# Two-layer graph network with two expert mixtures: the fused middle pass re-ordered, its answers halved on VectorE, weight loads moved and marked

## The chip, the cores and the metric

One core of one Trainium2 chip. The metric is the device time of one execution in microseconds (us), given as the median of three. Everything is float32; matrix products of the network run on the matrix engine (TensorE, PE), and the vector engine (VectorE, DVE), the scalar engine (ScalarE, ACT), GpSimd (POOL) and the DMA queues (SyncE's, written SPq, ScalarE's, written ACTq, and GpSimd's) feed it.

## What is computed

`x` holds 128 graphs of 64 nodes with 256 features, 8192 tokens in all, and `adj` an adjacency matrix of 64 x 64 for each graph. Cut to what matters, with `ln` a layer norm without weights:

```
# layer 0
n  = ln(x)
a  = epsilon*n + adj @ n
x1 = x + silu(rmsnorm(a @ W1 + b1)) @ W2 + b2          # 256 -> 1024 -> 256
n1 = ln(x1)
s, i = softmax_top6(n1 @ gate_w.T)                      # 6 of 64 experts for each token
m  = sum_k s_k * (n1 @ lattice[i_k])                    # each expert 256 x 256
x2 = x1 + layernorm(n1 + m @ out_w.T + out_b) * ln_g + ln_b
# layer 1
n2 = ln(x2)
h  = layernorm(n2) * gamma + beta
x3 = x2 + n2 + relu((adj @ h) @ W_rel + b_rel + h @ W_root)
n3 = ln(x3)
top2 of 8 experts by n3 @ Wg + bg + bias
out = x3 + sum over the 2 of w_e * (relu(n3 @ W1_e + b1_e) @ W2_e + b2_e)
```

## The kernel before

The tokens are cut into 32 blocks of 256 (`NB`), each held as two tiles of 128 rows (`T` = 2) with 256 columns (`KD` = 2 halves of 128). The kernel has four parts.

**First stage** (lines 496 to 727), one pass over the blocks: graph network of layer 0, gate, the six choices of each token. A `Router` gives each (token, choice) pair a row in a table in DRAM, and `send` writes the rows there with indirect DMAs from GpSimd. Memory is short: the tile `lat`, which will hold the 64 lattice experts, lends its upper 28 experts to this stage (weights, hidden values, x). `load_lattice` stands in the list for blocks 8 to 23 and fills the lower part, two experts (512 KB) a block; the rest is loaded after the stage. `load_late` issues the loads of constants and of W2 in the first step.

**Lattice pages** (729 to 782): 424 pages of 128 rows are fetched from the table, transposed, multiplied by the page's expert, scaled by the softmax weight and written by indirect DMA to the array `r0.answer`, six rows (`K0`) for each token.

**Fused pass** (785 to 998), where most of the change lies, one pass over the blocks. For each block:

- `load3` loads the six answers of each token as `y` (128 rows x 2 x 6 x 256), and the stored `xn1`, `x1` and adjacency.
- `mixture` transposes the answers on TensorE and adds the six in PSUM as it does so: 2 halves x 2 tiles x 6 answers = 24 transposes (line 828). ScalarE copies the sum to `accT`.
- `out_proj` multiplies by `out_w` into the PSUM tile `po` (lines 836, 839); `layer_out_h` adds `xn1` to it on VectorE and so frees `po` (845).
- `layer_out_a` takes mean and variance of `h` and lets ScalarE take the root (`spread`, line 36); `layer_out_b` normalises `h`, applies `ln_g`, adds `x1` (860, 862) and takes the statistics of the result `x2`; `layer_out_c` makes `hn` and `s` of it on ScalarE (879, 883).
- `flip_h` transposes `hn`; `neighbours` multiplies by `W_rel` (`pz`, 900) and ScalarE copies it to `z` (903); `convolve_a` adds bias and `W_root` product (`pc`, 908, 911); `convolve_b` applies the adjacency to `z` (917).
- `residual1_a` forms `x3` and its statistics (923); `residual1_b` normalises it twice over into `xs`; `flip3` and `gate1` transpose it and compute the gate (line 76, 946), ScalarE copying between them (940).
- `choose1` takes the two best experts (952 and on), `count1` counts the rows of each expert with small products (191), and `place1` computes the row numbers and sends `xs`.

**Expert pages** (1001 to 1060): 69 pages of 256 rows through the second mixture, added onto the output by indirect DMA.

The order of the work inside a pass is written out by hand. `staggered(n, stages)` runs step by step; in step s it calls each entry (lag, f) of a list, in the order of the list, for block s - lag. So in one step `mixture` works on block s+1 while `choose1` works on block s-3. TensorE, VectorE and ScalarE execute in exactly the order in which this produces the instructions (`manual_schedule`); the DMA queues of SyncE and the work of GpSimd are ordered by a scheduler that looks at what is ready.

PSUM of the fused pass: three rotating tiles `ps` for transposes, and one each of `po`, `pz`, `pc`, `pg` (gate) and `pos` (counts). A tile with one buffer is written again only when its reader is done. The list of the fused pass before:

```
(-2, load3), (0, layer_out_h), (3, choose1), (-1, mixture), (1, flip_h), (3, count1),
(2, residual1_a), (0, layer_out_a), (-1, out_proj), (2, residual1_b), (1, neighbours),
(0, layer_out_b), (1, convolve_a), (2, flip3), (1, convolve_b), (2, gate1),
(3, place1), (0, layer_out_c), (4, load_w2)
```

Of the kernel before, what the change touches and what calls it, by code (L numbers as in the profile page):

```python
# [9 lines left out]
F32 = mybir.dt.float32  # L10
# [5 lines left out]
AF = mybir.ActivationFunctionType  # L16
ALU = mybir.AluOpType
AX = mybir.AxisListType
PSUM = bass.MemoryType.PSUM
P = 128  # L20


def rows_of(vec, n=P):

    return bass.AP(tensor=vec.tensor, offset=vec.offset, ap=[[0, n], [1, vec.shape[0]]])
# [377 lines left out]
def staggered(n, stages, first=0):  # L403

    for s in range(first + min(lag for lag, _ in stages), n + max(lag for lag, _ in stages)):
        for lag, f in stages:
            if first <= s - lag < n:
                f(s - lag)
# [3 lines left out]
def two_layer_gnn_moe_kernel(ctx: ExitStack, tc: tile.TileContext, a: dict, out: bass.AP):  # L412
    nc = tc.nc
    x_in, adjT = a["x"], a["adjT"]
    N, D = x_in.shape
# [4 lines left out]
    T = 2  # L420
    C = T * P
# [4 lines left out]
    K0 = 6  # L426
# [14 lines left out]
        nc.gpsimd.memset(eps[v], v)  # L441
    ops = Ops(nc, small, ident, eps)

    def load_rows(pool, name):
        t = pool.tile([P, a[name].shape[0]], F32, name="r_" + name)
        nc.scalar.dma_start(out=t, in_=rows_of(a[name]))
        return t

    def load_columns(pool, name):

        t = pool.tile([P, a[name].shape[0] // P], F32, name="c_" + name)
        with nc.allow_non_contiguous_dma(reason="small vector"):
            nc.scalar.dma_start(out=t, in_=a[name].rearrange("(c p) -> p c", p=P))
        return t

    def load_matrix(pool, name):

        t = pool.tile([P, a[name].shape[0] // P, a[name].shape[1]], F32, name="m_" + name)
        nc.scalar.dma_start(out=t, in_=a[name].rearrange("(k p) f -> p k f", p=P))
        return t  # L460

    def row_parts(rest, name):
# [14 lines left out]
    def by_tile(ap):  # L477
        return ap.rearrange("(t p) d -> p t d", p=P)
# [8 lines left out]
    def load_adjacency(b):  # L487
        at = adjacency[b % 4]
        for g in range(2):
            nc.sync.dma_start(out=at[g * G:(g + 1) * G, :, g * G:(g + 1) * G],  # L490
                              in_=adjT[2 * b * T + g:2 * (b + 1) * T:2].rearrange("t m n -> m t n"))
        return at
# [3 lines left out]
    r0 = Router(tc, const, small, dram, N, D, E0, K0, T, P, 14 * P, 4, "r0")  # L496
# [3 lines left out]
    lat = lat_pool.__enter__().tile([P, E0, KD, D], F32, name="lat")  # L500
# [18 lines left out]
    with tc.tile_pool(name="c0", bufs=1) as c0, \  # L519
# [9 lines left out]
        blocks = [dict() for _ in range(NB)]  # L529
# [14 lines left out]
        w1 = w1_view.rearrange("p c n -> p (c n)").rearrange("p (k f) -> p k f", k=KD)  # L544
        nc.scalar.dma_start(out=w1, in_=a["L0_gnn_W1"].rearrange("(k p) f -> p k f", p=P))
        b1 = load_columns(c0, "L0_gnn_b1")
        w2 = w2_view
        late = {}

        def load_late(b):  # L550

            if b == 0:
                late["L0_gnn_b2"] = load_rows(c0, "L0_gnn_b2")
                late["rms_w"] = load_columns(c0, "L0_gnn_rms_weight")
                nc.scalar.dma_start(out=w2, in_=a["L0_gnn_W2"].rearrange("(k p) f -> p k f", p=P))
                late["gate_wT"] = load_matrix(c0, "L0_ffn_gate_wT")
                for name in ("L0_ffn_out_b", "L1_gnn_b_rel"):
                    late[name] = load_rows(c0, name)

        def split_late(b):  # L560
            if b < 3:
# [124 lines left out]
        def load_lattice(b):  # L686
            n = free[0] // 16
            if 8 <= b < 24:
                nc.sync.dma_start(out=lat[:, (b - 8) * n:(b - 7) * n], in_=lat_w[:, (b - 8) * n:(b - 7) * n])

        nc.scalar.preload_act_table_set("natural_log_exp_and_others")
# [18 lines left out]
            (0, square_sum),  # L710
            (-1, aggregate),
            (-1, load_late),
            (1, lambda b: project(b, 0, 4, KH)),
            (2, turn),
# [3 lines left out]
            (2, gate),  # L718
            (0, scale),
            (1, load_lattice),  # L720
        ))
        r0.page_table(sq.rearrange("p c n -> p (c n)"))
        n = free[0] // 16
# [65 lines left out]
    with tc.tile_pool(name="c3", bufs=1) as c3, \  # L789
            tc.tile_pool(name="work3", bufs=2) as work, \  # L790
            tc.tile_pool(name="ps3", bufs=3, space=PSUM) as psum, \
            tc.tile_pool(name="po3", bufs=1, space=PSUM) as po_pool, \
            tc.tile_pool(name="pm3", bufs=1, space=PSUM) as pmix:
        out_wT = load_matrix(c3, "L0_ffn_out_wT")
        ln_g = load_rows(c3, "L0_ffn_ln_g")
        ln_b = load_rows(c3, "L0_ffn_ln_b")
        gamma = load_columns(c3, "L1_gnn_ln_gamma")
        beta = load_columns(c3, "L1_gnn_ln_beta")
        w_rel = load_matrix(c3, "L1_gnn_W_rel")
        w_root = load_matrix(c3, "L1_gnn_W_root")  # L800
        wg = load_matrix(c3, "L1_ffn_Wg")
# [5 lines left out]
        blocks = [dict() for _ in range(NB)]  # L807
        pg = pmix.tile([P, T, E1], F32, name="pg")
        r1.begin(counts, work, pmix.tile([P, 2, T, E1], F32, name="pos"))

        def load3(b):
            B = blocks[b]
            B["y"] = y = work.tile([P, T, K0, D], F32, name="y")
            nc.sync.dma_start(out=y, in_=r0.answer[ts(b, C * K0), :].rearrange("(t p k) d -> p t k d", p=P, k=K0))
            B["xn1"] = xn1 = work.tile([P, T, D], F32, name="xn1", bufs=3)
            nc.sync.dma_start(out=xn1, in_=by_tile(xn1_dram[b]))
            B["x1"] = x1 = work.tile([P, T, D], F32, name="x1", bufs=3)
            nc.sync.dma_start(out=x1, in_=by_tile(x1_dram[b]))
            B["at"] = load_adjacency(b)

        def mixture(b):

            B = blocks[b]
            pt = psum.tile([P, KD, C], F32, name="ps")
            for k in range(KD):
                for t in range(T):
                    for i in range(K0):
                        nc.tensor.matmul(pt[:, k, ts(t, P)], lhsT=B["y"][:, t, i, ts(k, P)], rhs=ident,  # L828
                                         start=(i == 0), stop=(i == K0 - 1), is_transpose=True)
            B["accT"] = accT = work.tile([P, KD, C], F32, name="accT", bufs=1)  # L830
            nc.scalar.copy(accT, pt)

# [14 lines left out]
        def layer_out_a(b):  # L847
# [2 lines left out]
            B["rsh"] = ops.spread(B["mvh"])  # L850
            nc.vector.tensor_add(B["x1"], B["x1"], ln_b.unsqueeze(1).to_broadcast([P, T, D]))

        def layer_out_b(b):
            B = blocks[b]
            h = B["h"]
            mv, rs = B["mvh"], B["rsh"]
            nc.vector.reciprocal(rs, rs)
            B["x2"] = x2 = work.tile([P, T, D], F32, name="x2")
            for t in range(T):
                nc.vector.scalar_tensor_tensor(h[:, t, :], h[:, t, :], mv[:, t, 0:1], ln_g,  # L860
                                               op0=ALU.subtract, op1=ALU.mult)
                nc.vector.scalar_tensor_tensor(x2[:, t, :], h[:, t, :], rs[:, t:t + 1], B["x1"][:, t, :],
                                               op0=ALU.mult, op1=ALU.add)
            B["mv2"] = mv = ops.stats(x2)
            B["std2"] = ops.spread(mv)


            B["rs2"] = rs2 = small.tile([P, T], F32, name="rs2")
            ops.std(rs2, mv[:, :, 1], 1e-10, 1.0 + 1e-5)
# [93 lines left out]
        def place1(b):  # L963
            B = blocks[b]
            r1.send(r1.places(b, B["hot"]), B["xs"])

        staggered(NB, (
            (-2, load3),
            (0, layer_out_h),
            (3, choose1),  # L970
            (-1, mixture),
            (1, flip_h),
            (3, count1),
            (2, residual1_a),
            (0, layer_out_a),
            (-1, out_proj),
            (2, residual1_b),
            (1, neighbours),
            (0, layer_out_b),
            (1, convolve_a),  # L980
            (2, flip3),
            (1, convolve_b),
            (2, gate1),
            (3, place1),
# [103 lines left out]
```

## Time and profile before

| | before |
|---|---|
| time, median of 3 (lowest, highest) | 2461.87 us (2459.57, 2465.52) |
| the execution on the page | 2187.6 us, granted TensorE clock 0.959 |
| TensorE busy | 1947.8 us (89%) |
| VectorE busy | 1183.7 us (54%) |
| ScalarE busy | 1014.9 us (46%) |
| GpSimd busy | 1182.9 us (54%) |

| part of the kernel | TensorE from, to (us) | a unit of work |
|---|---|---|
| first stage | 9.9 to 650.3 | 32 blocks |
| lattice pages | 692.3 to 1222.1 | 424 pages |
| fused pass | 1257.7 to 1648.6 | 32 blocks |
| expert pages | 1660.8 to the end | 69 pages |

The timed executions took some 274 us longer than the one that the profiler recorded; the page covers the latter only. "Busy" is an average over four parts with different limits, so a stretch of one part says more than the first lines of the page. A group of instructions is written as line, engine, operation, output<-inputs, count, then busy time and mean of one, then the idle time of the engine just before and what ended it. The granted clock is 1.00 at full speed; 0.50 means that the matrix engine ran at half of it.

### The profile page before, as it was taken

The numbers are of one execution on the slowest core, as the hardware profiler recorded it, in microseconds if no ns is written. First come the engines' busy times: TensorE is split into PE (matmuls) and PEld (weight loads), VectorE is DVE, ScalarE is ACT, GpSimd is POOL, SyncE is SP. The second block draws the span as 40 slices with busy tenths as digits, with TensorE's granted clock in tenths as the row PEclk, the third lists the DMA queues.
The fourth block names the chain that finished last, engine by engine and source line by source line (L and its number), as shares of the span: only waits on it lengthen the run. The fifth ranks groups of instructions, "written<-read, shape, count | busy, mean of one in ns | idle before, by whom it ended". The sixth has DMA issues, their size and how long they took to land. (4 is left out here: it accounts for less than half of the span.)

```text
span 2185.7 us, 37432 instructions
## 1 busy us (share of the span) xinstructions
PE 1947.8 (89%) x10563; PEld 1686.4 (77%) x10564; DVE 1183.7 (54%) x3904; ACT 1014.9 (46%) x2037; POOL 1182.9 (54%) x1178
## 2 busy tenths in 40 slices
PE   5999999999943989998899389999986999999997
PEld 4887888888842877877777278888875888888886
DVE  4888888888873333333333258888882222222221
ACT  3887787778730222222222046666652333333332
POOL 1267666666665777777777603333343344334444
PEclk8999999999975999999999789999997999999999
DMA  8243333333365988667665379788835766666765
GB/s 250 79 133 130 134 132 134 128 132 132 118 215 166 278 255 253 206 205 205 206 206 167 100 286 310 261 260 264 267 119 152 178 157 168 159 153 164 163 159 118
DMA packets 283580, 398.93 MB, mean 183 GB/s; under 512 B 56024, under 2 KB 237416, under 8 KB 283376
## 3 DMA queue, kind: packets, MB, share of 16 engines
q1 hardware_dynamic: 200736, 246.15, 38.2%
q0 software_dynamic: 64800, 136.14, 20.9%
q10 hardware_dynamic: 17840, 14.21, 2.1%
q8 instruction: 93, 1.52, 0.3%
q14 instruction: 111, 0.91, 0.1%
HBM read 223.89 MB, written 177.69 MB: 184 GB/s over the span
## 5 line engine op out<-in xcount | busy, mean ns | idle before, releaser
L287 POOL DMA_INDIRECT r0x<-xs,r0row x384 | 398.5, 1038 | 209.7 <-issue 96.0
L294 POOL DMA_INDIRECT r0y<-py_s,px x424 | 417.5, 985 | 143.4 <-DMA r0y<-py_s,px 56.7
L768 PE MATMUL py<-lat,pxT 128*128 x1696 | 412.0, 386 | 40.8 <-DVE py_s L773 23.4
L773 DVE TENSOR_SCALAR py_s<-py,px 128x256 f32<-128x256 f32 x424 | 185.5, 479 | 376.8 <-DMA r0y<-py_s,px 152.2
L302 POOL DMA_INDIRECT out_x<-py_s,px x138 | 214.3, 1553 | 312.4 <-DMA out_x<-py_s,px 244.4
L768 PEld LDWEIGHTS py<-lat,pxT 128*128 128x128 f32 x1696 | 307.6, 191 | 92.9 <-ACT pxT L755 29.2
L755 ACT COPY pxT<-pt 128x512 f32<-128x512 f32 x212 | 123.8, 586 | 440.5 <-PE pt L753 342.0
L1027 ACT ACTIVATE phid<-ph,pw 128x256 f32<-128x256 f32 x276 | 130.7, 474 | 325.1 <-issue 181.6
L1025 PE MATMUL ph<-pxT,pw 128*128 128x256 f32 x1104 | 251.7, 381 | 1.7 <-DMA pw<-in_L_ffn_W1b 1.7
L1044 PE MATMUL py<-fw,phid 128*128 x1104 | 249.9, 379 | 0.3 <-issue 0.3
L599 PE MATMUL ph<-lat 128*128 128x256 f32 x1024 | 233.4, 387 | 17.9 <-DVE lat L621 17.2
L632 PE MATMUL ps<-lat 128*128 128x256 f32 x1024 | 237.5, 380 | 0.0
L1025 PEld LDWEIGHTS ph<-pxT,pw 128*128 128x128 f32 x1104 | 211.2, 191 | 31.1 <-ACT pxT L1016 2.0
L599 PEld LDWEIGHTS ph<-lat 128*128 128x128 f32 x1024 | 195.3, 193 | 47.4 <-DVE lat L621 17.5
L1044 PEld LDWEIGHTS py<-fw,phid 128*128 128x128 f32 x1104 | 204.4, 190 | 25.6 <-issue 0.5
L632 PEld LDWEIGHTS ps<-lat 128*128 128x128 f32 x1024 | 193.1, 191 | 24.6
L287 POOL DMA_INDIRECT r1x<-xs,r1row x128 | 129.6, 1012 | 116.7 <-ACT xn3T L940 62.7
L753 PE MATMUL pt<-ident,px 128*128 128x128 f32 x848 | 131.1, 278 | 43.1 <-DMA px<-r0x 42.7
L753 PEld LDWEIGHTS pt<-ident,px 128*128 128x128 f32 x848 | 107.1, 143 | 67.7 <-issue 43.2
L1038 DVE TENSOR_SCALAR p<-p 128x2 f32<-128x2 f32 x69 | 12.7, 184 | 242.8 <-ACT p L1037 242.8
L1047 DVE TENSOR_TENSOR py_s<-py,pb 128x512 f32<-128x512 f32 x69 | 47.7, 692 | 156.4 <-PE py L1044 151.4
L828 PE MATMUL ps<-ident,y 128*128 128x128 f32 x768 | 93.7, 281 | 38.6 <-DMA y<-r0y 38.6
(264 smaller groups left out, 2874.4 us busy)
## 6 DMA issues: line engine op xcount, KB each, us to landing
px<-r0x SPq DMA_DIRECT2D x424, 129.0 KB
y<-r0y SPq DMA_DIRECT2D x32, 1536.0 KB
pw<-in_L_ffn_W1b SPq DMA_DIRECT2D x69, 514.0 KB
px<-r1x SPq DMA_DIRECT2D x69, 258.0 KB
x<-x SPq DMA_DIRECT2D x64, 256.0 KB
pb<-in_L_ffn_b SPq DMA_DIRECT2D x69, 128.0 KB
r0x<-r0filler ACTq DMA_DIRECT2D x64, 129.0 KB
lat<-in_x SPq DMA_DIRECT2D x32, 256.0 KB
```

Source lines behind the costliest of these rows:

```text
L287: i = self.nc.gpsimd.indirect_dma_start(out=self.table[:, :], out_offset=bass.IndirectOffsetOnAxis(ap=row[:, t, k:k + 1], axis=0), in_=xs[ ...
L294: i = self.nc.gpsimd.indirect_dma_start(out=self.answer[:, :], out_offset=bass.IndirectOffsetOnAxis(ap=x[:, self.D:self.D + 1].bitcast(I32 ...
L302: i, d = f"{self.name}add{i}", self.nc.gpsimd.indirect_dma_start(out=self.total[:, :], out_offset=bass.IndirectOffsetOnAxis(ap=x[:, self.D ...
L599: nc.tensor.matmul(ph[:, c, :], lhsT=w1[:, k, ts(2 * j + c, P)], rhs=B["aggT"][:, k, :], start=(k == 0), stop=(k == KD - 1))
L632: nc.tensor.matmul(B["po"][:, t, :], lhsT=B["hT"][:, c, ts(t, P)], rhs=w2[:, c, :], start=False, stop=(t == T - 1 and c == KH - 1))
L753: nc.tensor.transpose(pt[:, k, ts(q, P)], Q["px", q][:, 0, ts(k, P)], ident)
L755: nc.scalar.copy(xT[:, :, :n * P], pt[:, :, :n * P])
L768: nc.tensor.matmul(py[:, q, :], lhsT=Q["xT"][:, k, ts(q, P)], rhs=lat[:, ds(regs["e"][(2 * j + q) % 4], 1), k, :].rearrange("p o d -> p (o ...
L773: nc.vector.tensor_scalar(y[:, q, :], py[:, q, :], px[:, 0, D + 1:D + 2], None, op0=ALU.mult)
L1025: nc.tensor.matmul(ph, lhsT=w[:, k * F1 + c * P:k * F1 + (c + 1) * P], rhs=Q["xT"][:, k, :], start=(k == 0), stop=(k == KD - 1))
L1027: nc.scalar.activation(hid[:, c, :], ph, AF.Relu, bias=w[:, KD * F1 + c:KD * F1 + c + 1], scale=1.0)
L1044: nc.tensor.matmul(py[:, t, :], lhsT=Q["hid"][:, c, ts(t, P)], rhs=fw2[:, ds(regs["e"][i % 4], 1), c, :].rearrange("p o d -> p (o d)"), st ...
```

## The change

Five edits, made together:

1. The constants, W2 and gate weights of `load_late` are issued on SyncE's DMA queue and no longer on ScalarE's.
2. Each `load_lattice` is preceded by a one-element memset by VectorE in the memory that it fills, a mark that keeps the scheduler from issuing the load before VectorE reaches that point of its order.
3. `halve`: VectorE adds answers 3 to 5 onto answers 0 to 2 before they are transposed, so that `mixture` needs 12 transposes and not 24. Loading of `y` is a stage of its own, a step earlier, with three buffers.
4. The normalising of `h` moves to ScalarE (`layer_out_n`), and `layer_out_b` on VectorE becomes one product and one sum over both tiles.
5. The list of the fused pass is in a new order: `residual1_a` and `choose1` stand ahead of `layer_out_h`; `count1` stands behind `out_proj`; `flip3` (the transposes for the gate) stands ahead of `convolve_a` (the root weights); `layer_out_a` stands behind `flip3`.

The aim is to take work off TensorE in the fused pass and to have less of it wait, and to free ScalarE at the start. The diff, cut to its core:

```diff
-    def load_rows(pool, name):
+    def load_rows(pool, name, engine=nc.scalar):
         t = pool.tile([P, a[name].shape[0]], F32, name="r_" + name)
-        nc.scalar.dma_start(out=t, in_=rows_of(a[name]))
+        engine.dma_start(out=t, in_=rows_of(a[name]))
         return t
...
         def load_late(b):
 
             if b == 0:
-                late["L0_gnn_b2"] = load_rows(c0, "L0_gnn_b2")
-                late["rms_w"] = load_columns(c0, "L0_gnn_rms_weight")
-                nc.scalar.dma_start(out=w2, in_=a["L0_gnn_W2"].rearrange("(k p) f -> p k f", p=P))
-                late["gate_wT"] = load_matrix(c0, "L0_ffn_gate_wT")
+                late["L0_gnn_b2"] = load_rows(c0, "L0_gnn_b2", nc.sync)
+                late["rms_w"] = load_columns(c0, "L0_gnn_rms_weight", nc.sync)
+                nc.sync.dma_start(out=w2, in_=a["L0_gnn_W2"].rearrange("(k p) f -> p k f", p=P))
+                late["gate_wT"] = load_matrix(c0, "L0_ffn_gate_wT", nc.sync)
                 for name in ("L0_ffn_out_b", "L1_gnn_b_rel"):
-                    late[name] = load_rows(c0, name)
+                    late[name] = load_rows(c0, name, nc.sync)
 
         def split_late(b):
             if b < 3:
...
         def load_lattice(b):
             n = free[0] // 16
             if 8 <= b < 24:
+
+                nc.vector.memset(lat[:1, (b - 8) * n, 0, :1], 0.0)
                 nc.sync.dma_start(out=lat[:, (b - 8) * n:(b - 7) * n], in_=lat_w[:, (b - 8) * n:(b - 7) * n])
 
         nc.scalar.preload_act_table_set("natural_log_exp_and_others")
...
         pg = pmix.tile([P, T, E1], F32, name="pg")
         r1.begin(counts, work, pmix.tile([P, 2, T, E1], F32, name="pos"))
 
+        def load_y(b):
+            blocks[b]["y"] = y = work.tile([P, T, K0, D], F32, name="y", bufs=3)
+            nc.sync.dma_start(out=y, in_=r0.answer[ts(b, C * K0), :].rearrange("(t p k) d -> p t k d", p=P, k=K0))
+
+        def halve(b):
+            y = blocks[b]["y"]
+            nc.vector.tensor_add(y[:, :, :K0 // 2, :], y[:, :, :K0 // 2, :], y[:, :, K0 // 2:, :])
+
         def load3(b):
             B = blocks[b]
-            B["y"] = y = work.tile([P, T, K0, D], F32, name="y")
-            nc.sync.dma_start(out=y, in_=r0.answer[ts(b, C * K0), :].rearrange("(t p k) d -> p t k d", p=P, k=K0))
             B["xn1"] = xn1 = work.tile([P, T, D], F32, name="xn1", bufs=3)
             nc.sync.dma_start(out=xn1, in_=by_tile(xn1_dram[b]))
             B["x1"] = x1 = work.tile([P, T, D], F32, name="x1", bufs=3)
...
             pt = psum.tile([P, KD, C], F32, name="ps")
             for k in range(KD):
                 for t in range(T):
-                    for i in range(K0):
+                    for i in range(K0 // 2):
                         nc.tensor.matmul(pt[:, k, ts(t, P)], lhsT=B["y"][:, t, i, ts(k, P)], rhs=ident,
-                                         start=(i == 0), stop=(i == K0 - 1), is_transpose=True)
+                                         start=(i == 0), stop=(i == K0 // 2 - 1), is_transpose=True)
             B["accT"] = accT = work.tile([P, KD, C], F32, name="accT", bufs=1)
             nc.scalar.copy(accT, pt)
 
...
             B["rsh"] = ops.spread(B["mvh"])
             nc.vector.tensor_add(B["x1"], B["x1"], ln_b.unsqueeze(1).to_broadcast([P, T, D]))
 
+        def layer_out_n(b):
+            B = blocks[b]
+            h = B["h"]
+            rs, nm = ops.scale_shift(B["mvh"], B["rsh"])
+            for t in range(T):
+                nc.scalar.activation(h[:, t, :], h[:, t, :], AF.Identity, bias=nm[:, t:t + 1], scale=rs[:, t:t + 1])
+
         def layer_out_b(b):
             B = blocks[b]
             h = B["h"]
-            mv, rs = B["mvh"], B["rsh"]
-            nc.vector.reciprocal(rs, rs)
             B["x2"] = x2 = work.tile([P, T, D], F32, name="x2")
-            for t in range(T):
-                nc.vector.scalar_tensor_tensor(h[:, t, :], h[:, t, :], mv[:, t, 0:1], ln_g,
-                                               op0=ALU.subtract, op1=ALU.mult)
-                nc.vector.scalar_tensor_tensor(x2[:, t, :], h[:, t, :], rs[:, t:t + 1], B["x1"][:, t, :],
-                                               op0=ALU.mult, op1=ALU.add)
+            nc.vector.tensor_mul(h, h, ln_g.unsqueeze(1).to_broadcast([P, T, D]))
+            nc.vector.tensor_add(x2, h, B["x1"])
             B["mv2"] = mv = ops.stats(x2)
             B["std2"] = ops.spread(mv)
 
...
             r1.send(r1.places(b, B["hot"]), B["xs"])
 
         staggered(NB, (
+            (-3, load_y),
             (-2, load3),
+            (-1, mixture),
+            (2, residual1_a),
+            (1, flip_h),
+            (3, choose1),
             (0, layer_out_h),
-            (3, choose1),
-            (-1, mixture),
-            (1, flip_h),
+            (-1, out_proj),
             (3, count1),
-            (2, residual1_a),
-            (0, layer_out_a),
-            (-1, out_proj),
             (2, residual1_b),
             (1, neighbours),
+            (2, flip3),
+            (0, layer_out_a),
+            (0, layer_out_n),
+            (-2, halve),
             (0, layer_out_b),
             (1, convolve_a),
-            (2, flip3),
             (1, convolve_b),
             (2, gate1),
             (3, place1),
```

More of the change, by code (lines that the diff above doesn't have):

```diff
@@ L442, in two_layer_gnn_moe_kernel, with load_columns, load_matrix @@
     ops = Ops(nc, small, ident, eps)
-    def load_rows(pool, name):
+    def load_rows(pool, name, engine=nc.scalar):
         t = pool.tile([P, a[name].shape[0]], F32, name="r_" + name)
-        nc.scalar.dma_start(out=t, in_=rows_of(a[name]))
+        engine.dma_start(out=t, in_=rows_of(a[name]))
         return t
-    def load_columns(pool, name):
+    def load_columns(pool, name, engine=nc.scalar):
         t = pool.tile([P, a[name].shape[0] // P], F32, name="c_" + name)
         with nc.allow_non_contiguous_dma(reason="small vector"):
-            nc.scalar.dma_start(out=t, in_=a[name].rearrange("(c p) -> p c", p=P))
+            engine.dma_start(out=t, in_=a[name].rearrange("(c p) -> p c", p=P))
         return t
-    def load_matrix(pool, name):
+    def load_matrix(pool, name, engine=nc.scalar):
         t = pool.tile([P, a[name].shape[0] // P, a[name].shape[1]], F32, name="m_" + name)
-        nc.scalar.dma_start(out=t, in_=a[name].rearrange("(k p) f -> p k f", p=P))
+        engine.dma_start(out=t, in_=a[name].rearrange("(k p) f -> p k f", p=P))
         return t
```

## The prediction

> **What bounds the kernel now.** I read the page's summary first, then engine time by stretches, then the chain of waits inside one block of the fused pass, and last the rows and the start that the edits touch. Stretches (window and length, then busy us of PE, PEld, DVE, ACT, POOL with counts, granted clock, DMA share, GB/s):
>
> ```profile
> 0.00:100.00 100.00, 76.71 (x364) 65.41 (x365) 61.64 (x175) 59.84 (x122) 14.29 (x42) 0.91 0.56 170
> ...
> 200.00:300.00 100.00, 94.96 (x532) 83.09 (x532) 89.60 (x275) 81.21 (x163) 68.64 (x71) 1.00 0.40 132
> ...
> 1450.00:1500.00 50.00, 50.00 (x327) 43.61 (x325) 44.16 (x193) 32.04 (x67) 19.92 (x23) 1.00 0.82 260
> ```
>
> The fused pass lies at 1258 to 1649 us; in it TensorE is never idle and VectorE is close behind. The chain of waits over one block (start, us, what):
>
> ```profile
> 1439.15 0.44 PE ps L76 x4
> 1439.90 1.97 PE po L839 x8
> 1441.87 1.73 PE pz L900 x8
> 1443.81 1.73 PE pc L911 x8
> 1445.54 0.44 PE ps L76 x4
> 1445.97 0.87 PE pc L917 x4
> 1446.84 0.92 PE pg L946 x8
> 1447.76 2.67 PE ps L828 x24
> 1450.44 0.44 PE ps L76 x4
> ```
>
> It holds nothing but TensorE and repeats after 1450.44 - 1439.15 = 11.29 us: today's period. VectorE's only steady wait there is this (count | busy, mean ns | idle before, releaser):
>
> ```profile
> L952 DVE TENSOR_TENSOR logits<-pg,r_L_ffn_bg 128x16 f32<-128x16 f32 x27 | 4.7, 174 | 17.4 <-PE pg L946 17.4
> ```
>
> 17.4/27 = 0.64 us a block, so VectorE occupies 10.65 of the 11.29 (gaps between its instructions included). At the start of the kernel (start, us, engine, idle before in brackets):
>
> ```profile
> 25.05 1.57 ACT L602 ACTIVATE lat<-ph,c_L_gnn_b 128x256 f32<-128x256 f32 x4 [12.49 <-DMA at<-in_adjT]
> ...
> 27.53 2.08 PE L589 MATMUL ps<-at,lat 128*128 128x128 f32 x8 [6.20 <-DVE lat L581]
> ```
>
> ScalarE issues the late constants from 16.70 to 24.55 us and squares nothing before 25.05, though the first `ph` was begun at 12.61.
>
> [...] work was ready behind ScalarE's DMA issues and did not pass. [...] in the first blocks of the fused pass, on the same 24 transposes:
>
> ```profile
> 1268.13 4.51 PE L828 MATMUL ps<-ident,y 128*128 128x128 f32 x24 [2.97 <-DMA y<-r0y]
> ...
> 1275.20 2.78 PE L828 MATMUL ps<-ident,y 128*128 128x128 f32 x24
> ```
>
> [...] 512 elements take 701 ns and 1024 take 1251 ns (the adds of L609 from 200 to 500 us), 1.07 ns an element.
>
> **The change part by part, fused pass.** (a) The transposes of `mixture` go from 24 to 12: 2.67/24 x 12 = 1.33 us a block off TensorE, whose sum becomes 9.96.
>
> (b) `halve` adds one tensor_add of 1536 elements on VectorE, which the trace lacks: 1251 + 512 x 1.07 = 1.80 us; some 0.1 of it overlaps the next instruction, as in neighbouring rows: 1.70.
>
> (c) `layer_out_n` and the new `layer_out_b`: four scalar_tensor_tensor go (1441.90 to 1443.72, 1.82 us) and a reciprocal (0.07); two 512-element operations (0.60 each from start to start), a reciprocal and a small product (0.30) come. Two ScalarE activations of `h` (0.55 each, as L879) are new. VectorE: 10.65 + 1.70 - 1.89 + 1.50 = 11.96 us, already above 11.29.
>
> (d) The new order. This is the part that counts. The instructions of the changed program stand on each engine in this order. TensorE: `mixture`(s+1), `flip_h`(s-1), `out_proj`(s+1), counts, `neighbours`(s-1), `flip3`(s-2), `convolve_a`, `convolve_b`, `gate1`. ScalarE: ..., z copy (after `neighbours`), xn3T copy (after `flip3`), only then the square root of `layer_out_a`(s), then `h`. VectorE: `residual1_a`(s-2), `choose1`(s-3), `layer_out_h`(s), ..., `layer_out_a`(s), `layer_out_n`(s), `halve`(s+2), `layer_out_b`(s), `place1`, `layer_out_c`. Three waits close a ring. `out_proj`(s+1) writes the only `po` buffer and waits for `layer_out_h`(s), which now stands third on VectorE. The root of `layer_out_a`(s) queues on ScalarE behind copies that wait for `neighbours` and `flip3`, which TensorE runs after `out_proj`(s+1). And `layer_out_n`(s) on VectorE waits for that root, with `halve`, the layer norm, `place1`, `layer_out_c` and the next block's `residual1_a`, `choose1` and `layer_out_h` queued behind. In the kernel before, `layer_out_h` was first and the root stood ahead of the z copy, so no such ring was closed.
>
> Its length, from `layer_out_h`(s) to `layer_out_h`(s+1), by starts in the timeline of 1439 to 1451 us. TensorE: bias 0.22, output projection 1.83, counts 0.11, `neighbours` 1.73, `flip3` to its end 0.60: 4.49. ScalarE: xn3T copy 0.59, root 0.30: 0.89. Four hand-overs between engines of about 0.08: 0.3. VectorE: scale and shift 0.30, `halve` 1.70, product and sum 1.20, statistics 1.08, `place1` 0.97, `layer_out_c` 0.74, `residual1_a` 1.81, `choose1` 1.59, `layer_out_h` 0.69: 10.08. Sum 15.8 us against 11.29: +4.5. ScalarE's `h` (1.1) hides under `halve`, its next roots under `place1`.
>
> (e) TensorE then idles 15.8 - 10.0 = 5.8 us a block, in two pieces (waiting for hn at `flip_h`, then for `layer_out_h` at `out_proj`) with only 0.44 of work between. By the 4.51 against 2.78 row such a gap brings half clock for about 3.7 us of work afterwards, and what follows it is `out_proj` and `neighbours`, on the ring. At most 3.7/2 = 1.9 us are lost; I take 1.5, since part may fall on `flip_h` or be missed: period 17.3. Ends: 0 (15.8) and all 4.49 at half clock (20.3).
>
> The ring binds in some 30 of the steps: 30 x (17.3 - 11.3) = +180 us. Before it `halve` adds 1.8 to the path to the first `mixture`: +2. The third y buffer and separate `load_y` cost nothing: DMA share falls with the longer period.
>
> **First stage.** The late constants move from ScalarE's queue to SyncE's, and the 1-element memsets hold the lattice loads (16 of 512 KB, all issued by 38 us before) back to blocks 8 to 23. ScalarE is free at 12.6 and can square from about 15; the mean-square sum could end near 25 instead of 33.7 (product at 33.75 us). I take -9 us, bounds 0 (w2 and the constants, now ahead of the second adjacency on SyncE, delay it as the lattice did) and -13. The lattice's 8 MB fall where the DMA share is 0.40, hidden by the matmuls. Sixteen memsets at 0.1 us on VectorE: +1.
>
> Sum: 180 + 2 - 9 + 1 = +174. The page's execution took 2187.6 us, the timed ones 2461.87; no view shows the difference, and I add the change as it stands: 2461.87 + 174 = 2636. Were the difference a slower TensorE, today's period would be longer in timed runs too and the ring worth less, some 3.2 x 30 = +96: 2550.
>
> **The rivals.**
> 1. TensorE stays the bound and the change does what it is for: -1.33 x 32 = -43, with -9: 2410. For it: TensorE 50.00 of 50.00 us busy. Against it: VectorE's 11.96 alone exceed today's period. This one is faster.
> 2. VectorE is the bound without any ring: 0.67 x 32 = +21, with -6: 2477. For it: 44.16 of 50 busy. Against it: the root behind the z copy in a first-in queue.
> 3. The ring at full clock: 30 x 4.5 = 135, with -6: 2591. [...]
> 4. The ring with TensorE at half clock throughout: 30 x 9 = 270, with -6: 2726.
>
> **How the numbers follow.** Ring with part half clock 0.60; rival 3 0.23; rival 4 0.07; rival 2 0.05; rival 1 0.05. The range reaches from below rival 3, towards the case of a slower TensorE, to short of rival 4: 2565 to 2705, leaving out rivals 1, 2 and 4 (0.17). Faster 0.05 is rival 1; same 0.02 and 0.03 of slower are shares of rival 2; slower in all 0.93.
>
> **What would show it.** In the changed profile a block of the fused pass should take 16 to 18 us; the reciprocal of `layer_out_n` should show some 4 us idle before it, released by ScalarE; `out_proj` and `flip_h` should idle 2 to 3.5 us before their first matmul; the clock in that pass should be below 1.00. In the first stage ScalarE's first squares should start near 15 us. I am wrong if the period stays at 12 or less, or if TensorE stays busy throughout.

## The result and the profile after

The kernel after takes 2600.55 us in the median of 4 executions (2599.47 to 2620.79), the kernel before 2463.69 us beside it: a ratio of 1.0572 (95% interval 1.0516 to 1.0629), +137 us.

A caution on the chips first. The executions fall into two groups by the chip that ran them: on one chip the kernel before takes 2186 us (e1 to e4 below), on two others 2464 and 2468 us (e5 to e8, and e9 to e11). Each chip was used at one time only, so chip and time are not told apart. The profile shown of before is of the first group; its timed executions and all executions of the kernel after are of the second. So each comparison below is with before on the same chip.

Stretches of 100 us of the kernel after (window and length, then busy us of PE, PEld, DVE, ACT, POOL with counts, granted clock, DMA share, GB/s); the first lies in the first stage, the others in the fused pass:

```profile
200.00:300.00 100.00, 80.61 (x406) 68.80 (x405) 71.07 (x220) 63.28 (x122) 55.91 (x59) 0.91 0.38 126
1600.00:1700.00 100.00, 71.18 (x369) 58.04 (x367) 65.77 (x257) 46.63 (x100) 23.67 (x29) 0.81 0.51 170
1800.00:1900.00 100.00, 70.88 (x351) 57.56 (x352) 64.57 (x254) 47.34 (x100) 25.11 (x30) 0.80 0.53 175
```

In the fused pass no engine is full any more: TensorE is busy 71 of 100 us at a clock of 0.80, VectorE 65. Something other than work sets the time. The chain of waits over one block of the kernel after (start, us, what):

```profile
1713.75 0.70 DVE x L933
...
1717.22 0.61 DVE h L853
1717.88 0.61 PE po L844
1718.48 2.84 PE po L847 x8
1721.40 1.84 PE pz L910 x8
1723.33 0.40 ACT z L913
1723.81 0.59 ACT xn3T L950
1724.40 0.20 ACT bn_sd L36
1724.63 0.18 DVE bn_rs L67
1724.83 0.16 DVE bn_nm L68
1724.99 1.67 DVE y L819
1726.65 0.61 DVE h L872
1727.29 0.70 DVE x L873
...
1730.82 0.70 DVE x L933
```

It goes from VectorE to TensorE to ScalarE and back to VectorE, and returns to the same instruction after 1730.82 - 1713.75 = 17.07 us. Such a chain, which comes back to its start one block later, is called a ring here. Most blocks of the pass take 17.1 us; some near its start and around 1790 us take 17.2 to 18.6, and the expectations below have their 17.8 from one of those. Before, the chain stayed on TensorE, for 11.29 us a block. What the engines waited for on this path, from the timeline of the kernel after (start, us, engine, line, operation; in brackets the idle time before and what ended it):

```profile
1714.05 1.39 PE L76 MATMUL ps<-ident,hn 128*128 128x128 f32 x4 [2.49 <-ACT hn L889]
...
1717.88 0.61 PE L844 MATMUL po<-p_L_ffn_out_b,r1ones 128*128 128x512 bf16 x1 [2.43 <-DVE h L853]
...
1724.63 0.17 DVE L67 RECIPROCAL bn_rs<-bn_sd 128x2 f32<-128x2 f32 x1 [4.88 <-ACT bn_sd L36]
```

TensorE stands still 2.49 us for `hn` and, after 1.4 us of transposes, 2.43 us for `layer_out_h`; VectorE stands still 4.88 us for the root that queues behind ScalarE's copies.

The granted clock follows the blocks. Three stretches, cut where it changes (columns as above; the clock stands third from the end):

```profile
1703.53:1713.77 10.24, 8.03 (x53) 7.02 (x51) 5.80 (x21) 3.21 (x8) 0.22 (x1) 1.00 0.26 76
1713.77:1720.60 6.83, 4.10 (x11) 2.87 (x12) 5.59 (x25) 4.80 (x10) 3.96 (x4) 0.50 0.96 338
1720.60:1730.84 10.24, 8.03 (x53) 7.02 (x51) 5.80 (x21) 3.21 (x8) 0.22 (x1) 1.00 0.23 64
```

It is full for 10.24 us and half for 6.83, 17.07 together: one block. `out_proj` (1717.88 to 1721.32) falls almost whole into the half.

In the first stage the squares (L602) now begin at 15.9 us; before, at 25.0 (first and last start behind the range of durations):

```profile
L602 ACT ACTIVATE lat<-ph,c_L_gnn_b x256: 454/473/487, 15.9 to 744.1; 128x256 f32<-128x256 f32 x128
```

### The profile page after: what moved, and what is told of

Its sections match the earlier page's. It is cut to its first block, busy times and chain, and to the rows that moved or that the text cites. A ratio compares the mean times of both kernels' runs of the same rounds, so it can differ in the third digit from the quotient of the medians.

```text
span 2597.6 us, 36890 instructions
## 1 busy us (share of the span) xinstructions
PE 2072.3 (80%) x10180; PEld 1740.0 (67%) x10180; DVE 1226.2 (47%) x3920; ACT 1043.1 (40%) x2101; POOL 1175.4 (45%) x1178
## 4 chain that ended last, share of the span: by engine, by line
PE 38%; DVE 15%; issue 8%; DMA 5%; ACT 3%; another core or an unknown queue 3%; SPq 2%; POOL 2%; ACTq 0%; DVEq 0%; POOLq 0%
PE py L770 9%; PE ph L1038 9%; PE py L1057 9%; PE po L847 3%; PE pt L755 3%; PE pz L910 2%; DVE y L819 2%; DVE bn_st L45 2%; DMA out_x<-py_s,px 1%; SPq L397 1%; DMA px<-r0x 1%; DVE py_s L775 1%; PE pt L76 1%; DMA r0y<-py_s,px 1%
## 5 line engine op out<-in xcount | busy, mean ns | idle before, releaser
L770 PE MATMUL py<-lat,pxT 128*128 x1696 | 439.4, 402 | 56.5 <-issue 37.6
L775 DVE TENSOR_SCALAR py_s<-py,px 128x256 f32<-128x256 f32 x424 | 177.0, 478 | 472.0 <-PE py L770 158.7
L770 PEld LDWEIGHTS py<-lat,pxT 128*128 128x128 f32 x1696 | 323.2, 201 | 111.5 <-issue 54.1
L632 PE MATMUL ps<-lat 128*128 128x256 f32 x1024 | 275.3, 420 | 8.1 <-issue 6.8
L632 PEld LDWEIGHTS ps<-lat 128*128 128x128 f32 x1024 | 217.9, 216 | 48.7 <-issue 13.8
L755 PE MATMUL pt<-ident,px 128*128 128x128 f32 x848 | 146.2, 287 | 100.1 <-DMA px<-r0x 81.1
L602 ACT ACTIVATE lat<-ph,c_L_gnn_b 128x256 f32<-128x256 f32 x256 | 103.5, 471 | 129.6 <-remote 70.2
L76 PE MATMUL ps<-ident,xs 128*128 128x128 f32 x256 | 48.0, 315 | 93.7 <-ACT lat L592 85.3
```

The costliest lines, as they stand in the source:

```text
L632: nc.tensor.matmul(B["po"][:, t, :], lhsT=B["hT"][:, c, ts(t, P)], rhs=w2[:, c, :], start=False, stop=(t == T - 1 and c == KH - 1))
L755: nc.tensor.transpose(pt[:, k, ts(q, P)], Q["px", q][:, 0, ts(k, P)], ident)
L770: nc.tensor.matmul(py[:, q, :], lhsT=Q["xT"][:, k, ts(q, P)], rhs=lat[:, ds(regs["e"][(2 * j + q) % 4], 1), k, :].rearrange("p o d -> p (o ...
L775: nc.vector.tensor_scalar(y[:, q, :], py[:, q, :], px[:, 0, D + 1:D + 2], None, op0=ALU.mult)
```

## The experiments

"Pass" below is the time from the first to the last gate product of the fused pass in the profile (31 block intervals). Medians stand beside before's on the same chip.

| run | median us | before | ratio (95%) | pass us | before's pass |
|---|---|---|---|---|---|
| e1_before_again | 2187.61 | 2186.42 | 1.0004 (0.9995 to 1.0013) | 346.4 | 346.4 |
| e2_root_ahead | 2224.59 | 2186.42 | 1.0184 (1.0161 to 1.0206) | 384.3 | 346.4 |
| e3_start_only | 2181.00 | 2186.42 | 0.9985 (0.9968 to 1.0002) | 346.4 | 346.4 |
| e4_fused_only | 2365.32 | 2186.42 | 1.0832 (1.0814 to 1.0850) | 518.8 | 346.4 |
| e5_after_again | 2601.64 | 2464.44 | 1.0550 (1.0488 to 1.0612) | 518.9 | 387.3 |
| e6_order_only | 2547.89 | 2464.44 | 1.0345 (1.0284 to 1.0405) | 468.0 | 387.3 |
| e7_halve_gpsimd | 2482.34 | 2464.44 | 1.0073 (1.0051 to 1.0096) | 395.9 | 387.3 |
| e8_more_transposes | 2595.95 | 2464.44 | 1.0538 (1.0475 to 1.0601) | 519.4 | 387.3 |
| e9_both_gaps | 2562.31 | 2468.34 | 1.0394 (1.0367 to 1.0421) | 478.4 | 387.3 |
| e10_fold_one | 2439.75 | 2468.34 | 0.9892 (0.9871 to 0.9912) | 366.8 | 387.3 |
| e11_before_control | 2461.62 | 2468.34 | one execution | 387.3 | 387.3 |

Before's pass of 387.3 us is from e11's profile, of the chip of e9 and e10; it stands in for the chip of e5 to e8, of which there is no profile of before. The kernel after has a pass of 519.3 us in its own profile.

**e1 and e11: before, unchanged, on either chip.**

> The kernel before, unchanged, recorded again. Its page showed 2187.6 us while its timed executions took 2461.87; the changed kernel's page (2597.6 us) agrees with its timed ones, and shows first-stage and lattice-page stretches with waits that nothing visible ends ('remote', 'issue'). Theory A (those waits are a state that timed executions of both kernels share): a new record of the kernel before shows about 2460 us, with the same waits and TensorE below full clock in the first 1200 us, and the fused pass still at 11.3 us a block. Theory B (edits 1 and 2 make them): the record stays near 2187 us with no such waits.

> The kernel before beside these two on their chip. The fused pass took 346 us from the first to the last gate product in both earlier records of it (2187 us in all). Where timed executions take about 2460 us: if waits that nothing visible ends also lie in its fused pass, that pass is 25 to 45 us longer here, which would explain that the changed kernel's disadvantage is 137 us there against 179 us of the fused edits where before takes 2186; if the pass is 346 us again, the missing 40 us are in the other stages.

e1 gives 2187.61 us and the pass of the page, 346.4; e11 gives 2461.62 and a pass of 387.3. So the 274 us between the page and the timed executions go with the chip. e1 alone fits theory B, but theory B is wrong: e11 shows long waits of the kind "remote" (an unseen source) in the first stage (before the squares of L602 they are 48.9 us in 13, the longest 6.9) without edits 1 and 2, and e3 below shows none of them with these edits. The 274 us lie in three parts: the first transpose of the lattice pages (L753) comes 142 us later (833.8 in e11, 692.2 on the page), these pages take 110 us longer (to 1463.6, and to 1212.5), and the pass is longer by 41; some 18 us are regained in between. The chain of waits of e11 in the fused pass:

```profile
1743.15 1.99 PE po L839 x8
...
1753.71 0.44 PE ps L76 x4
1754.15 1.08 PE pos L191 x4
1755.23 0.02 issue
1755.25 0.59 ACT accT L831
1755.84 0.04 issue
1755.89 1.99 PE po L839 x8
```

The period is 1755.89 - 1743.15 = 12.74 us, not 11.29: TensorE waits about 1.4 us a block for `accT`, whose copy begins 1.5 us after the last transpose has ended (1753.71); on the other chip it begins 0.1 us after (1439.24 on the page). The trace puts the copy's wait down to the counts (`pos`), which it does not read; SyncE's load of the next `y`, which waits for the same transposes, is also issued 1.5 us after them (1755.19). The clock is 1.00. So the kernel before is not wholly bound by TensorE on the chips where it was timed.

**e3 and e4: the change in two.** e3 has the load edits and the marks alone, e4 all the rest.

```diff
 # e3: before, with
-                nc.scalar.dma_start(out=w2, in_=...)
+                nc.sync.dma_start(out=w2, in_=...)
...
+                nc.vector.memset(lat[:1, (b - 8) * n, 0, :1], 0.0)
 # e4: after, without these lines
```

> The kernel before with only edits 1 and 2 (late constants on SyncE's queue, lattice loads marked). My step: 9 us less than before, by an earlier first square (near 15 us), bounds 0 to 13; the fused pass stays at 11.3 us a block. Rival (the edits make the first stage slower, as its longer stretch in the changed kernel's record suggests): over 50 us more than before.

> The changed kernel with edits 1 and 2 undone: only halving, normalising on ScalarE and the new order are left. If the parts add up as predicted, the fused pass keeps its 17.8 us a block and the time is 9 us above the changed kernel's, about 2610. If edits 1 and 2 made the first stage slower, it is 50 us or more below it.

e4 is 2365.32 - 2186.42 = +178.9 us, e3 is -5.4, with an interval that includes no change. The first stage ends 6.3 us earlier in e3's profile than in e1's (642.3 against 648.6). The sum is +173.5. e4's pass is 172.4 us longer than before's, so nearly all of the loss lies in the fused pass. The 2610 of e4's expectation was reckoned for the other chips; its pass has the length that it has in after.

**e5: after again**, as the control of its chip.

> The changed kernel, unchanged, beside the kernel before on the same chip. If the parts add up (e3 5 us below before, e4 179 us above), about 2359 us, 174 above before, and the fused pass at 17.8 us a block; if the first-stage waits of its first record belong to the kernel, about 2600 us again.

Its pass is 518.9 us, as long as e4's 518.8 on the other chip. Before's pass depends on the chip, after's does not. The time is near the second figure of the expectation, but not for the reason given there: the first-stage waits are in e11 too, so they are not of the changed kernel alone.

**e6: only the new order**, with 24 transposes and VectorE normalising as before.

```diff
 # before, with the list
+            (-1, mixture), (2, residual1_a), (1, flip_h), (3, choose1), (0, layer_out_h),
+            (-1, out_proj), (3, count1), (2, residual1_b), (1, neighbours), (2, flip3),
+            (0, layer_out_a), (0, layer_out_b), (1, convolve_a), (1, convolve_b), (2, gate1), ...
```

> The kernel before with only the new order of the fused pass: 24 transposes, normalising on VectorE, no halving, no other edit. Ring theory: the ring without halve and with the old layer_out_b is 4.49 + 0.89 + 0.3 + 8.8 = 14.5 us, with some loss of clock 14.5 to 15.5, so 100 to 130 us above before. Rival (halving is what costs, the order is neutral): within 15 us of before's 2186.

+83.5 us of the +137 come with the order alone. The expected 100 to 130 were reckoned from before's pass of 346 us; the pass is 121.6 us longer than that one, and 80.7 longer than the 387.3 of the other chips. Its waits from 1600 to 1950 us (engine, what it waited to write, for what: us in total, times, longest):

```profile
DVE bn_sd L857 <- ACT bn_sd L36: 106.2, 23, 6.7
...
PE po L836 <- DVE h L845: 61.3, 22, 2.8
```

106.2/23 = 4.6 us a block on VectorE for the root and 2.8 on TensorE for `layer_out_h`: the same two waits as after. The order closes the ring. The other edits add the remaining 51 us of the pass (518.9 - 468.0); that `halve` and `layer_out_n` do so by lengthening the ring was predicted, and fits the chain of after, but was not run one by one.

**e2: the root moved out of the ring**, two entries of the list and nothing else.

```diff
+            (0, layer_out_a),
+            (0, layer_out_n),
             (1, neighbours),
             (2, flip3),
-            (0, layer_out_a),
-            (0, layer_out_n),
             (-2, halve),
```

> The changed kernel with layer_out_a and layer_out_n moved ahead of neighbours and flip3, nothing else. Ring theory: ScalarE no longer takes the root behind the z and xn3T copies, the ring opens, the 5.6 us wait of the reciprocal behind bn_sd is gone, and the period of the fused pass falls from 17.8 to 12 to 13 us (VectorE's sum of 11.96 then bounds it), 30 x 5 = about 150 us less than the changed kernel. Rival (halving itself, as load on VectorE, costs the time): the period stays above 16 us and the time within 30 us of the changed kernel's 2600.

The pass falls from 518.8 (e4) to 384.3 us. The chain of e2 (start, us, what):

```profile
1410.06 1.05 ACT xs L943 x2
1411.10 0.38 issue
1411.48 0.29 ACT bn_sd L36
1411.77 0.02 issue
1411.79 0.18 DVE bn_rs L67
1411.99 0.16 DVE bn_nm L68
1412.15 1.67 DVE y L819
...
1424.50 1.67 DVE y L819
```

TensorE is no longer on it: the root stands behind `xs` and not behind copies that wait for TensorE, and the period is 1424.50 - 1412.15 = 12.35 us (in each third block some 13.1). VectorE is busy 90.2 to 91.0 of 100 us. This is near the bound that the prediction gave for VectorE, 11.96, but a shorter way from VectorE to ScalarE (`xs`, the root) and back is left on the chain, so VectorE's work is not all that sets it. It is above before's 11.29: with TensorE off the chain, this version with halving on VectorE is still slower than before on that chip.

**e8 and e9: the clock's share.** e8 does the 12 transposes of `mixture` three times over, e9 moreover the 4 of `flip_h` five times. The repeats write the same values again, so nothing is left out; TensorE has 24 and 40 more transposes a block to do, while the ring's own work stays the same.

```diff
 # e8: after, with
-            for k in range(KD):
-                for t in range(T): ...
+            for _ in range(3):
+                for k in range(KD):
+                    for t in range(T): ...
 # e9: and with
-            ops.transpose(pt, B["hn"])
+            for _ in range(5):
+                ops.transpose(pt, B["hn"])
```

> The changed kernel with mixture's 12 transposes of a block done three times over (the last one counts): TensorE has 24 transposes, 2.67 us at full clock, more to do, most of it in the gap in which it waits for hn. Clock theory (the ring is 15.8 us at full clock and stretched to 17.8 by half clock after the gaps): the granted clock of the fused pass rises from 0.80 towards 1.00, the projection's 8 matmuls fall from 3.6 us towards 2.0, the period from 17.8 to 16 to 16.7, and the time by 30 to 55 us. Rival (clock has no part in the ring): period and time stay or rise by up to 2.7 x 30 = 80 us.

> As e8 (mixture three times over), and flip_h's four transposes done five times over as well, so that TensorE has work in both gaps, ahead of flip_h and ahead of out_proj: 40 transposes or 4.4 us a block more than in the changed kernel. e8 left the gap of 2.8 us ahead of out_proj and its period stayed at 17.8. Clock theory: with no gap left over 1 us the clock is 0.97 or more in the fused pass, the projection's 8 matmuls end 2.0 us after their start and not 3.5, and the period is 15.8 to 16.4, so 40 to 60 us less than the changed kernel although TensorE does more. Rival (the projection is slow for another reason): the period stays at 17.8 or rises.

e8 missed its expectation: the pass is 519.4 us, not shorter. Its timeline says why:

```profile
1765.98 0.61 PE L845 MATMUL po<-p_L_ffn_out_b,r1ones 128*128 128x512 bf16 x1 [2.79 <-DVE h L854]
1766.38 3.04 PE L848 MATMUL po<-m_L_ffn_out_wT,accT 128*128 128x256 f32 x8
```

The wait before `flip_h` is gone, and the mean clock rises from 0.80 to 0.90, but the wait before `out_proj` is left, and what follows it is on the ring: eight matmuls in 3.04 us, as in after. The clock is now at half for 3.41 us of each block instead of 6.83, and just there: from 1765.29 to 1768.70. In e9 (timeline again, one block):

```profile
1746.43 0.39 PE L845 MATMUL po<-p_L_ffn_out_b,r1ones 128*128 128x512 bf16 x1 [1.03 <-DVE h L854]
1746.65 1.89 PE L848 MATMUL po<-m_L_ffn_out_wT,accT 128*128 128x256 f32 x8
```

the wait is 1.03 us and the same eight take 1.89. The chain of e9:

```profile
1742.30 0.70 DVE x L935
...
1746.82 1.73 PE po L848 x8
...
1758.03 0.70 DVE x L935
```

Its period is 15.73 us with a granted clock of 1.00 up to the last blocks of the pass: the ring at full clock. So of the 17.07, 1.34 are clock, 41 us over the pass (519.4 - 478.4). TensorE does 40 more transposes a block than in the kernel after, and the loss is 94.0 us, not e8's 131.5 or e5's 137.2.

The kernel after and e8 have the same period, 17.07 us, although e8 does 24 more transposes. Both traces show the clock change in steps of 3.41 us, and 17.07 is five of them. Before the clock falls to half, TensorE was busy for 1.20 us (after) and 1.16 us (e8) of a step; in e9 it is busy for 2.38 us or more of each step from 1751 to 1779 us, and the clock stays. It looks as if the ring locks onto these steps; no run tested why it settles at five.

**e7: halving on GpSimd**, in an order without the ring.

```diff
-            nc.vector.tensor_add(y[:, :, :K0 // 2, :], ...)
+            nc.gpsimd.tensor_add(y[:, :, :K0 // 2, :], ...)
 # and the list: mixture, layer_out_h, layer_out_a, flip_h, residual1_a, layer_out_n, choose1,
 # residual1_b, convolve_a, neighbours, layer_out_b, count1, out_proj, halve, flip3, ...
```

> The changed kernel with halve on GpSimd and an order without the ring: layer_out_h and layer_out_a ahead of flip_h, layer_out_n before choose1, out_proj behind layer_out_b, flip3 behind it. If order and VectorE's load are all that is wrong, the sums bound it: VectorE 10.26, TensorE 9.96, so 10.3 to 11 us a block and 15 to 35 us below before's 2186. If GpSimd's add (not seen in any trace so far) is slow enough to delay mixture, or slows VectorE, the period is above 11.3 and the time above 2181.

It is 17.9 us slower than before. One block of its timeline:

```profile
1850.15 3.44 POOL L819 TENSOR_TENSOR y<-y 128x1536 f32<-128x1536 f32 x1
...
1850.63 3.51 DVE L859 TENSOR_TENSOR x<-x,r_L_ffn_ln_b 128x512 f32<-128x512 f32 x1
```

VectorE's add of 512 elements, 0.66 us elsewhere (L851 in e11's timeline), is recorded at 3.51: it ends 0.55 us after GpSimd's add (1854.14 against 1853.59). This add is the one stretched in 10 of the 32 blocks. In 19 others it is another VectorE instruction, in nine of them a conversion of 0.17 us (L181) that takes 3.1 us. What holds VectorE's instruction up while GpSimd adds, the trace does not name. VectorE loses 80.5 us over the pass so, 2.5 us a block, more than the 1.67 that it was spared. The pass is longer than before's by 8.6 us; where the other 9 of the 17.9 lie was not followed up.

**e10: a cheaper fold, and no ring.** Only answer 5 is added onto answer 4, so 20 transposes stay and VectorE's add has 512 elements; normalising stays on ScalarE, and the root and `layer_out_n` stand early in the list.

```diff
-            nc.vector.tensor_add(y[:, :, :K0 // 2, :], y[:, :, :K0 // 2, :], y[:, :, K0 // 2:, :])
+            nc.vector.tensor_add(y[:, :, K0 - 2, :], y[:, :, K0 - 2, :], y[:, :, K0 - 1, :])
 # list: layer_out_h, layer_out_a, flip_h, mixture, residual1_a, layer_out_n, choose1, residual1_b,
 # neighbours, halve, out_proj, layer_out_b, count1, flip3, place1, convolve_a, convolve_b,
 # layer_out_c, gate1
```

> A version that may beat both: edits 1 and 2, normalising on ScalarE, VectorE folds only one of the six answers onto another (512 elements, 0.65 us) so that 20 transposes stay, and an order without the ring (layer_out_h and layer_out_a first, out_proj behind the next block's root). Sums: TensorE 11.29 - 0.44 = 10.85, VectorE 10.26 + 0.65 = 10.9: 10.9 to 11.1 us a block, 6 to 12 us less in the fused pass and 5 less at the start, so 0.5 to 0.8% below before. Rival (another ring or queue binds): 11.5 us or more a block, not below before.

2439.75 us against before's 2468.34: 28.6 us faster than before, and faster than after. A stretch of its fused pass:

```profile
1700.00:1800.00 100.00, 90.94 (x578) 78.33 (x579) 86.63 (x360) 66.14 (x143) 35.89 (x41) 1.00 0.75 246
```

TensorE is 91% busy and VectorE 87% at full clock, and the pass is 366.8 us against 387.3. A block takes 12.1 us, not the expected 10.9 to 11.1, so the sums do not bound it: TensorE waits about 0.7 us a block for `accT`, and VectorE as long for a root. The expected gain was 0.5 to 0.8% and the measured one is 1.1%, on a chip where before's own pass is 41 us longer than on the page; some 8 of the 28.6 us lie outside the pass. It was run only where before takes 2464 us; on the other chip, where before's TensorE never waits in a full step of the pass, its gain is not known. Nor was it shown which of its parts brings it.

## Why the prediction was right, point by point

**(a) to (c), the work moved.** `halve` lies on the chain for 1.67 us, predicted 1.70. TensorE's transposes fall as counted, and it is no use: TensorE isn't the bound after. VectorE's bound without a ring, 11.96 predicted, stands against 12.35 in most blocks of e2, with VectorE some 91% busy.

**(d), the ring.** Right in path and size. The chain shows each link in the order given, e2 opens it by moving two entries and gets back 134 us of the pass (518.8 - 384.3), and at full clock it is 15.73 us (e9) where 15.8 was summed from before's rows.

**(e), the clock.** Right in kind and size; 1.5 us was taken and 1.34 measured. The rows show where it goes: `po` 2.84 rather than 1.73 in e9, its bias 0.61 rather than 0.39, 1.33 together; `pz` is at full clock (1.84). "Part may fall on `flip_h`" came true: its four transposes take 1.39 us at half clock, and they are not on the chain. The bound of 1.9 is a little high: 4.51 against 2.78 is a loss of 1.73. The period is 17.07, predicted 17.3. What the prediction did not see is that the ring and the steps of the clock fall together, so that the waits lie at the same place of a step in block after block.

**The number of steps.** 30 full steps were taken, and 30 x (17.07 - 11.29) = 173 us. The pass grows by 519.3 - 346.4 = 173 us. e4 is +178.9 in time, predicted +182 for the fused pass; the 6 us outside the pass were not followed up.

**The first stage.** -9 predicted, bounds 0 and -13, with the marks +1; e3 measured -5.4 in the median, not told apart from 0, and 6.3 us earlier in the profile. The squares start at 15.9 us, predicted near 15. Of the 9 us that ScalarE gains some 6 reach the end of the stage; where the rest goes was not followed up.

**The sum.** +174 predicted; e3 and e4 add to +173.5 on the chip of the page, closer than the two terms (+182 and -8 against +178.9 and -5.4), whose errors cancel. On the chips of the timed executions it is +137. The mis-sized term is "I add the change as it stands": the 2461.87 hold a fused pass of 387 us and not 346, because before itself waits about 1.4 us a block there, while after's chain does not contain that wait. 519.3 - 387.3 = 132 is nearly all of the 137. The text named this case ("today's period would be longer in timed runs too and the ring worth less"), with the wrong cause: not a slower TensorE, since the clock is 1.00 in e11's pass, but a late hand-over to `accT`. So 2636 was 35 us too high, inside the range. That the range held is in part luck: the effect shrank by some 40 us for a cause that the prediction did not have, and the time came out nearer to rival 3 (2591). The time alone does not tell the two apart; the clock of 0.80 and e9 do.

**The signs.** Block 17.1 us (16 to 18 named), 4.88 us idle before the reciprocal (some 4 named), 2.49 and 2.43 before `flip_h` and `out_proj` (2 to 3.5 named), clock 0.80: all present. Of the rivals, 1 and 2 fell with the period. Rival 3 (full clock; its 0.23 was the author's estimate) is e9, a kernel with more work on TensorE, and not after; rival 4 (half clock throughout) fell with the 0.80.

**What stays open.** Why the chips differ: before's copy to `accT`, the first stage and the lattice pages all start later there. The trace puts the waits down to an unseen source, to issuing or, for `accT`, to an instruction that the copy does not need. No run took that apart. Nor was it shown why the ring settles at five steps of the clock.

## What to carry to other kernels

Before re-ordering a list that several engines execute in order, follow each buffer with a single copy and each short operation behind another engine's results once around: if the way returns to its start in the next block, its sum is a lower bound of the period, however little the engines have to do. Here the order alone cost 83 us, and moving two entries gave most of the loss back. Where such a ring holds short waits of TensorE, look at the granted clock beside it: work added on one of two waits gave nothing, on both it took 41 us off the pass. Work taken off the fullest engine pays only up to the next engine's bound: a version that folds one answer onto another, in an order without the ring, gained, where those that fold three did not; which of its parts brought the gain is open.

## What the runs showed of the hardware

- More work made the kernel faster: 40 extra transposes a block took the loss from 137 to 94 us (e9), since TensorE kept its full clock (1.00 against 0.80).
- The granted clock changes in steps of 3.41 us: full for 10.24 us and half for 6.83 in most blocks of after, 13.65 and 3.41 in e8, 40.96 and 3.41 late in e6. A step need not be idle throughout for half clock to follow: in after TensorE was busy for 1.20 of the 3.41 us before the clock fell (1710.36 to 1713.77) and for 1.38 of the next 3.41, about its waits of 2.49 and 2.43 us; it was busy for 2.72 of the step behind these, and then the clock was full again (from 1720.60).
- So a wait of the same length costs time or not by where it falls. In e6 TensorE waits 2.79 us before `out_proj` in block after block; in its chain of waits the eight matmuls behind it take 1.73 us at 1702.54 and at 1732.68 us, and 2.58 at 1716.78 in between. How much of a step has to be idle, no run was made to show.
- In e9 TensorE does only transposes from 1754.4 to 1762 us, busy for 6.57 of the 7.60 us, a wait of 1.33 us begins there, and the granted clock is 1.00 then and after. In the kernel before it does only transposes in the half-clock step from 1268.46 to 1271.87 us, and the next step is at full clock. So the clock stayed up in the one and came back in the other behind transposes alone.
- GpSimd's add of 1536 float32 elements took 3.44 us (VectorE: 1.67). In 29 of 32 blocks of e7 one VectorE instruction of 0.16 to 0.69 us was stretched, to 4.14 us at most, and ended 0.01 to 0.55 us after that add.
- One and the same kernel took 2186 us on one chip and 2464 to 2468 on two others, each used at one time.
